# A graph layer's edge sums: groups owned by their middle edge, sums in two parts, Newton steps on ScalarE

## The chip, the cores and the metric

The kernel runs on one core of one Trainium2 chip. The metric is the device time of one launch in microseconds, as the median of several runs. A core has five engines with a queue each: TensorE (PE, with its weight loads shown apart as PEld), VectorE (DVE), ScalarE (ACT), GpSimd (POOL) and SyncE (SP, which issues DMAs). Each works its queue strictly in the order in which the program wrote it, and waits where the next instruction is not ready. DMAs are issued from SP, ACT or POOL.

## The reference, cut to what matters

There are 625 nodes of 512 features, 20,625 edges sorted by their target node (10,000 random edges in both directions, and a loop on each node), and 4 kinds of edges with a 512x512 matrix each.

```python
h = max(layernorm(x), 0)                       # 625 x 512
for r in range(4):
    w_r = where(edge_type == r, edge_weight, 0)
    total_msg += (h[src] @ W_rel[r] + b_rel[r]) * w_r[:, None]
agg = segment_sum(total_msg, dst)              # sum over the edges of each target
deg = segment_sum(edge_weight, dst)
agg = agg / max(deg, 1)[:, None]
z   = h + (h @ W_self + b_self + agg)
x1  = layernorm(z) * ln1_g + ln1_b
ffn = gelu(x1 @ W_ffn1 + b_ffn1) @ W_ffn2 + b_ffn2     # 512 -> 1024 -> 512
out = x + layernorm(x1 + ffn) * ln2_g + ln2_b
```

## The kernel before

**Blocks and the table.** The nodes stand in five blocks of 128 rows (0 to 4), 640 rows for 625 nodes; the 15 rows too many are a gap at the end of block 1 (rows 241 to 255), which so has 113 nodes. The first stage makes a table of 4 x 640 rows in memory: each block's transposed h times each kind's matrix, plus the bias (`table_rows`, matmuls at L404, the copy out of PSUM with its scale at L417, the store at L419). An edge's message is then one row of this table times its weight. While TensorE does this, VectorE works out columns of indices and weights (`outer_columns`, `group_columns` L757, `degree_columns`), one-hot tiles for the degrees, and for block 0 and part of block 4 the cells of a count matrix, which POOL scatters to memory (L687).

**Two ways to sum edges.** Blocks 0 and 4 (the outer ones) have a dense matrix of edge weights, node by table row (`sums_w`); their sums are 20 matmuls with it each, L1302, where the table comes back in chunks by DMAs from SP (`chunk_load`, L1297). The rest of block 4's matrix is made by `outer_sum` (L614), whose banks VectorE and ScalarE empty (L557 to L567). The blocks 1 to 3 and the tiles at the boundaries to the outer blocks gather rows: an indirect DMA on POOL (`gather`, L1159) brings 128 table rows for 128 edges into one of ten buffers `ms`.

**Groups of three.** Of the gathered tiles, 90 form 30 groups of three (`EG` = 3): partition p of a group's three tiles holds three consecutive edges, which nearly always have the same target. The group's owner is the target of its first edge. ScalarE scales the first row (`first_row`, L1165, into one of two PSUM buffers `add`), VectorE adds the second and the third, each with its weight where its target is the owner's, else with zero (`row_added`, L1183, weights `wgt_g` from L761). So three gathered tiles cost one product with a one-hot matrix, which takes the 128 sums to their nodes (`edge_sum`, L1201). The nine single tiles go straight from `ms` into a product, with the weight in their one-hot matrix (L1194).

**Two forms of a product.** A whole product takes fp32 operands; it shows as two matmul instructions. Where `parted` (L1175) says so, the sum is cut in two: a high part in fp32r, cast on ScalarE (`high`, L1169), and the rest as a low part, on VectorE (`low`, L1173); TensorE then does two fp32r matmuls, one behind the other, as one step of the order (L1205, L1206). Before the change that is the first two of every three groups of a set, but for the last three units of the last set.

**Stray rows.** At the border between two nodes a group can hold edges of both. An edge that is not the owner's is left out by its zero weight, and added by itself: up to two for each node, so two gathers for each of the blocks 1 to 3 (`gather_first`, L1214, six in all). `first_edges`, `first_rows` and `first_found` (L794 to L824) find them; VectorE adds these rows to z directly (`add_first`, L1211, the instruction is at L430).

**Sets, and the order.** The gathered tiles fall in sets by the blocks that they reach, in this order: (3,4) and (0,1) with 4 single tiles each; (1) with 8 groups; (1,2) with 2; (2) with 9; (2,3) with 2; (3) with 9 groups and one single tile. Each set has one PSUM accumulator `acc`, which VectorE adds to z at its end (L430). When a block's sums are complete, its norm runs (`first_norm`: L881 to L893; the inverse root by a guess and three Newton steps on VectorE, `rsqrt_steps`, L869 and L870, for block 3 by a power on POOL), its x1 is turned by TensorE (L352) and copied by ScalarE (L1365), and its feed-forward follows (`up` L925, gelu L931, `down` L945, a second norm L955 to L970, the store L996 and L998). The blocks go through it in the order 0, 4, 1, 2, 3. `self_part` (L442) is the h @ W_self of each block.

**What sets the order.** From the table's end on, the program lists operations with an engine, an estimated time, what they come after, and counted buffers that they take and give back (class `Plan`). A list scheduler in the program gives each engine a fixed order from it; at run time only the waits decide. The constants `MS`, `ES`, `OW`, `LAND` and the like are buffers and estimates of that plan. `spin` (L1226) are empty matmuls that keep TensorE's clock up.

## Time and profile before

| | us |
|---|---|
| median of 3 runs | 259.0 (258.2 to 260.4) |
| the profiled execution | 258.17 |
| its span | 256.3 |
| granted TensorE clock, mean | 0.998 |
| table stage (TensorE on L404) | 9.9 to about 84 |
| gathers issued on POOL | 88 to 222, 99 and 6 |
| feed-forward of block 3 and the end | 233.5 to 256.3 |

The span runs from the first to the last instruction of one execution. An engine's busy time counts its instructions; a TensorE that is busy isn't always at its peak. Where a row shows brackets, they hold the idle time of the engine just ahead of it and what ended it. In groups, the numbers behind the bar are busy us and the mean ns of one, then the idle time ahead.

### The profile page before, as it was taken

Reading aid. Unit: us, or ns where it says so; the run is one execution under the profiler, and the core shown is the slowest. Engines: PE = TensorE matmul, PEld = TensorE weight load, DVE = VectorE, ACT = ScalarE, POOL = GpSimd, SP = SyncE. Lnnn points to the kernel's source line nnn. Section 1 sums busy time; section 2 is a strip of 40 time slices with the busy share of each in tenths; the row PEclk is TensorE's granted clock in tenths of the full one; section 3 lists DMA queues with packets and bytes.
Section 4 is the critical chain, followed back from the end, with each engine's and each line's share of the span. In section 5 each row is a group of like instructions: output and inputs, shape, how many; then the busy total and the mean of one; then the engine's idle time right before and its main releaser. Section 6 shows DMA issues by size and latency. Waiting matters only on the chain.

```text
span 256.3 us, 3522 instructions
## 1 busy us (share of the span) xinstructions
PE 243.2 (95%) x1051; PEld 140.0 (55%) x1051; DVE 199.6 (78%) x501; ACT 79.3 (31%) x236; POOL 170.6 (67%) x230
## 2 busy tenths in 40 slices
PE   7999999999999979999995999999899999999993
PEld 6354444445445644444442445875775766847872
DVE  3797899998899974646968879997969999776232
ACT  3117400000032463713231314571542451502500
POOL 4378888888888477777777777777777777501000
PEclk9999999999999999999999999999999999999999
DMA  6999999882172399799999887677777776720101
GB/s 205 320 405 415 377 393 400 289 337 79 51 247 89 110 374 388 207 306 320 372 309 375 285 263 205 191 209 215 208 214 220 235 206 194 214 79 0 45 0 45
DMA packets 24055, 60.20 MB, mean 235 GB/s; under 512 B 4401, under 2 KB 8753, under 8 KB 22882
## 3 DMA queue, kind: packets, MB, share of 16 engines
q0 software_dynamic: 9936, 27.58, 34.9%
q1 hardware_dynamic: 13808, 30.94, 32.8%
q10 hardware_dynamic: 290, 1.44, 1.7%
q8 instruction: 9, 0.15, 0.2%
q14 instruction: 12, 0.10, 0.1%
HBM read 50.78 MB, written 9.17 MB: 234 GB/s over the span
## 4 chain that ended last, share of the span: by engine, by line
PE 54%; DMA 26%; DVE 9%; issue 4%; ACT 2%; POOL 1%; SPq 1%; POOLq 0%; DVEq 0%; ACTq 0%
PE ps L404 22%; DMA ms<-table,row_i 17%; PE ps L925 8%; PE acc L1302 6%; PE ps L945 5%; PE acc L1208 4%; PE ps L442 3%; DMA wr<-in_L_gnn_W_rel_dram 2%; DMA sums_w<-cells 2%; DMA ms<-table,x_row 2%; DVE add L1183 2%; PE spin L1226 2%; POOL ms L1159 1%; DMA cells<-weight,cell 1%; PE add L787 1%
## 5 line engine op out<-in xcount | busy, mean ns | idle before, releaser
L1159 POOL DMA_INDIRECT ms<-table,row_i x99 | 96.3, 972 | 30.9 <-issue 14.0
L404 PE MATMUL ps<-wr,hT 128*128 128x512 f32 (+2 forms) x168 | 71.2, 576 | 0.2 <-DMA wr<-in_L_gnn_W_rel_dram 0.2
L687 POOL DMA_INDIRECT cells<-weight,cell x45 | 48.3, 1073 | 9.0 <-issue 6.3
L404 PEld LDWEIGHTS ps<-wr,hT 128*128 128x128 f32 x168 | 30.7, 191 | 34.0 <-issue 30.4
L1183 DVE SCALAR_TENSOR_TENSOR add<-ms,wgt_g,add 128x512 f32<-128x512 f32 x51 | 38.0, 748 | 5.8 <-DMA ms<-table,row_i 3.1
L925 PEld LDWEIGHTS ps<-x1T,w_sb 128*128 128x128 f32 x320 | 37.3, 191 | 4.7 <-issue 2.4
L925 PE MATMUL ps<-x1T,w_sb 128*128 128x128 f32 (+2 forms) x320 | 37.8, 275 | 1.3 <-ACT x1T L1365 1.2
L1165 ACT ACTIVATE add<-ms,ed 128x512 f32<-128x512 f32 x30 | 20.7, 691 | 51.5 <-DMA ms<-table,row_i 42.3
L945 PE MATMUL ps<-w_sb,gT 128*128 128x512 f32 (+3 forms) x96 | 36.2, 522 | 0.0
L600 ACT ACTIVATE ohw<-os,w 128x128 fp32r<-128x128 f32 x36 | 11.3, 389 | 56.1 <-DVE os L582 56.1
L1302 PE MATMUL acc<-tr,sums_w 128*128 128x512 f32 x60 | 27.9, 595 | 0.0
L945 PEld LDWEIGHTS ps<-w_sb,gT 128*128 128x128 f32 (+1 forms) x96 | 16.6, 188 | 14.2 <-issue 11.4
L442 PE MATMUL ps<-ws_sb,hT 128*128 128x512 f32 x40 | 18.6, 592 | 0.0
L931 ACT ACTIVATE gT<-ps,bf 128x128 f32<-128x128 f32 (+1 forms) x40 | 13.9, 364 | 11.0 <-PE ps L925 10.1
L1302 PEld LDWEIGHTS acc<-tr,sums_w 128*128 128x128 f32 x60 | 11.0, 189 | 11.5 <-issue 10.5
L1173 DVE TENSOR_TENSOR el<-add,eh 128x512 fp32r<-128x512 f32 x21 | 14.3, 683 | 2.8 <-ACT eh L1169 2.8
L1169 ACT CAST eh<-add 128x512 fp32r<-128x512 f32 x21 | 12.2, 582 | 12.5 <-DVE add L1183 11.2
L1205 PE MATMUL acc<-eh,oh 128*128 128x512 f32 x21 | 13.2, 628 | 0.5 <-DVE z L430 0.5
L417 DVE SCALAR_TENSOR_TENSOR tr<-ps,rx,brel_bc 128x512 f32<-128x512 f32 x15 | 11.1, 743 | 3.0 <-PE ps L404 3.0
L442 PEld LDWEIGHTS ps<-ws_sb,hT 128*128 128x128 f32 x40 | 7.6, 190 | 8.0 <-issue 7.7
L1206 PE MATMUL acc<-el,oh 128*128 128x512 f32 x21 | 8.8, 418 | 2.9 <-DVE el L1173 2.8
L955 DVE TENSOR_TENSOR ow<-ps,z 128x512 f32<-128x512 f32 (+3 forms) x6 | 3.6, 596 | 10.2 <-PE ps L945 10.1
(215 smaller groups left out, 301.4 us busy)
## 6 DMA issues: line engine op xcount, KB each, us to landing
tr<-table SPq DMA_DIRECT2D x11, 512.0 KB, 6.6
w_sb<-in_L_gnn_W_ffn_dram SPq DMA_DIRECT2D x2, 2048.0 KB, 10.2
table<-tr SPq DMA_DIRECT2D x15, 256.0 KB, 6.2
wr<-in_L_gnn_W_rel_dram SPq DMA_DIRECT2D x3, 1024.0 KB, 9.5
cells<-zeros SPq DMA_DIRECT2D x2, 1280.0 KB, 11.2
ms<-table,row_i POOLq DMA_INDIRECT x99, 3.8
rows<-in_rows_dram SPq DMA_DIRECT2D x1, 1536.0 KB, 13.1
sums_w<-cells ACTq DMA_DIRECT2D x1, 1280.0 KB, 6.5
```

What stands on the lines that cost most here:

```text
L404: nc.tensor.matmul(p_[:, :h.stop - h.start], hT[i][:, k, :], wr_sb[r][:, k, h], start=(k == 0), stop=(k == KD - 1))
L442: nc.tensor.matmul(p[0], hT[i][:, k, :], ws_sb[:, k, :], start=(k == 0), stop=(k == KD - 1))
L687: s = nc.gpsimd.indirect_dma_start(out=cells[i][:, :], out_offset=bass.IndirectOffsetOnAxis(ap=cell[i][:, k:k + 1], axis=0), in_=weight[i] ...
L925: nc.tensor.matmul(pu[:, :nn + first], w1_sb[:, k, f * P:(f + 1) * P], x1T_b()[:, k, :nn + first], start=(k == 0), stop=(k == KD - 1))
L931: nc.scalar.activation(box["gT"][:, f, :nn], pus[f][:, :nn], AF.Gelu, bias=bf1[:, f:f + 1])
L945: nc.tensor.matmul(po[h][:n, :w], box["gT"][:, f, at], w2_sb[:, f, c], start=(f == 0), stop=(f == KF - 1))
L1159: nc.gpsimd.indirect_dma_start(out=ms[j], out_offset=None, in_=table[:, :], in_offset=bass.IndirectOffsetOnAxis(ap=row_i[:, j:j + 1], axis=0))
L1165: nc.scalar.activation(box["sum"], ms[j], AF.Copy, scale=wgt[:, j:j + 1])
L1173: nc.vector.tensor_sub(box["low"], box["sum"], box["high"].bitcast(F32))
L1183: nc.vector.scalar_tensor_tensor(to, ms[j], wgt_g[:, k, q - 1:q], box["sum"], op0=ALU.mult, op1=ALU.add)
L1205: nc.tensor.matmul(acc[bs], ohs[0][:, q, :], box["high"], start=(k == 0), stop=False)
L1302: nc.tensor.matmul(acc[b,], sums_w[b][:, c, :], kept[(b, c) if (b, c) in kept else c], start=first, stop=last)
```

## The change

1. **The owner of a group is its middle edge's target.** The weights `wgt_g` now exist for all three rows, zero where a row's target is not the middle's. At a border inside a group only the first or only the last row is then a stray one, so there is one stray row per border: one gather per block, three in all, chosen by `chosen`. The degree columns keep the old, first-edge owner (`wgt_1`).
2. **A block's stray rows are a tile of their own set.** Each of (1), (2), (3) begins with them: the row with its weight in two parts, times a one-hot matrix `x_hots` made in `first_found`. The direct additions to z are gone.
3. **The gap moves** to rows 255 to 269: block 1 has 127 nodes, block 2's begin at its row 14. The sets become (1) 9 groups, (1,2) 2, (2) 8, (2,3) 2, (3) as before. The feed-forward works on all 128 rows of each block.
4. **Most sums go in two parts:** all of every set but the last, single tiles too (`high_of_row`, `low_of_row`, straight from `ms`); of the last set every second unit, but for its last three. A whole sum's third addition writes into its `ms` buffer.
5. **The products of the parts are steps of their own in the plan,** and any order between the first and the last of a set is allowed. High and low parts get rings of their own (4 and 3 buffers, in place of 7 shared ones); the ring `ow` goes from 5 to 4.
6. **Newton steps:** in the first norm of blocks 0, 1, 2 and 4, and in the second of blocks 0, 4, 1 and 2, the three steps are on ScalarE, three instructions each; the guess stays on VectorE.

```diff
-        self.gap_at = 2 * P - self.gap
+        self.gap_at = 2 * P - 1
-        self.size = [P - (self.gap if b == 1 else 0) for b in range(nb)]
+        self.rows = [(self.gap - 1 if b == 2 else 0, P - (b == 1)) for b in range(nb)]
...
     def group_columns():
         first = grouped(dst_f)[:, :, 0:1].to_broadcast([P, GROUPS, EG - 1])
-        nc.vector.scalar_tensor_tensor(wgt_g, grouped(dst_f)[:, :, 1:], 0.0, first, op0=ALU.add, op1=ALU.not_equal,
+        middle = grouped(dst_f)[:, :, EG // 2:EG // 2 + 1].to_broadcast([P, GROUPS, EG])
+        nc.vector.tensor_tensor(wgt_1, grouped(dst_f)[:, :, 1:], first, op=ALU.is_equal)
+        nc.vector.tensor_mul(wgt_1, wgt_1, grouped(wgt)[:, :, 1:])
+        nc.vector.scalar_tensor_tensor(wgt_g, grouped(dst_f), 0.0, middle, op0=ALU.add, op1=ALU.not_equal,
                                        accum_out=x_missing)
-        nc.vector.tensor_tensor(wgt_g, grouped(dst_f)[:, :, 1:], first, op=ALU.is_equal)
-        nc.vector.tensor_mul(wgt_g, wgt_g, grouped(wgt)[:, :, 1:])
+        nc.vector.tensor_tensor(wgt_g, grouped(dst_f), middle, op=ALU.is_equal)
+        nc.vector.tensor_mul(wgt_g, wgt_g, grouped(wgt))
...
         nc.tensor.matmul(first[:, :INNER], before, counts[:, 1:], start=True, stop=False)
+        nc.tensor.matmul(first[:ep.rows[2][0], 1:2], behind, counts[:, 2:3], start=False, stop=False)
...
+        nc.vector.scalar_tensor_tensor(x_step, x_cols[:, :, :, 2], float(NP), x_cols[:, :, :, 0], op0=ALU.mult, op1=ALU.add)
+        chosen(x_row, x_step, x_one[:, 0, :])
+
+    def chosen(to, of, t):
+
+        nc.vector.tensor_sub(t, of[:, :, 0], of[:, :, 2])
+        nc.vector.tensor_mul(t, t, x_on[:, :, 0])
+        nc.vector.tensor_add(to, t, of[:, :, 2])
+
+    def first_found():
+
+        dst, t, ok = (x_one[:, i, :] for i in (1, 2, 3))
+        chosen(dst, x_cols[:, :, :, 1], t)
+        nc.vector.tensor_max(ok, x_on[:, :, 0], x_on[:, :, 1])
...
+        chosen(t, x_edges[:, :, :, 3].bitcast(F32), x_one[:, 0, :])
+        nc.vector.tensor_mul(x_one[:, 0, :], t, ok)
+        nc.vector.tensor_tensor(x_hots, dst.unsqueeze(2).to_broadcast([P, INNER, P]),
+                                node_row[:, :P].unsqueeze(1).to_broadcast([P, INNER, P]), op=ALU.is_equal)
...
         def improve(three):
             v, y, a = col(0), col(1), col(2)
+            if on == "ACT":
+                nc.scalar.activation(a, y, AF.Square)
+                nc.scalar.activation(a, a, AF.Copy, scale=v, bias=-three)
+                nc.scalar.activation(y, a, AF.Copy, scale=y)
+                return
...
-    ES = 7
+    EH, EL = 4, 3
-    OW = 5
+    OW = 4
-    PARTED = 2, 3
+    WHOLE = 3
+    POW, ROOTS = 0.9, (("ACT", "ACT", "ACT", "POOL", "ACT"), ("ACT",) * 5)
...
     def parted(bs, k, units):
-        return len(units[k]) > 1 and k % PARTED[1] < PARTED[0] and (k + 3 < len(units) or bs != order_of[-1])
+        return (k % 2 == 0 and k + WHOLE < len(units)) or bs != order_of[-1]
...
+    def high_of_row(j, ms, box):
+        box["high"] = buffer("eh")
+        nc.scalar.activation(box["high"], ms[j], AF.Copy, scale=weight_of(j))
+
+    def low_of_row(j, ms, box):
+        box["low"] = buffer("el")
+        nc.vector.scalar_tensor_tensor(box["low"], ms[j], weight_of(j), box["high"].bitcast(F32),
+                                       op0=ALU.mult, op1=ALU.subtract)
...
         if q == EG - 1 and not parts:
-            to = edge.tile([P, D], F32, tag="es", name=f"es_{j}", bufs=ES)
-        nc.vector.scalar_tensor_tensor(to, ms[j], wgt_g[:, k, q - 1:q], box["sum"], op0=ALU.mult, op1=ALU.add)
+            to = ms[j]
+        nc.vector.scalar_tensor_tensor(to, ms[j], wgt_g[:, k, q:q + 1], box["sum"], op0=ALU.mult, op1=ALU.add)
...
+    def products(bs, passes, last, q, ohs, box, j, needs, give, rank):
+
+        for part in ("high", "low") if "low" in needs else ("sum",):
+            first = not passes
+            passes.append(op("PE", 0.87 if part == "sum" else 0.235,
+                           lambda first=first, part=part, end=last and part != "high": edge_sum(
+                               bs, first, end, q, ohs, lambda: box[part] if part in box else ms[j]),
+                           after=[needs[part], needs["hots"], *(passes if last and part != "high" else passes[:1])], take=["acc"] if first else [],
+                           give=give[part], lag=0.25, rank=rank, level=0.25))
+        return passes[-1]
...
-        for b in range(1, NB - 1):
-            if bs == ((b, b + 1) if b < NB - 2 else (b,)):
-                for q in range(EG - 1):
-                    g_last = op("POOL", GATHER, lambda b=b, q=q: gather_first(b, q, ms), after=[g_last, rows_of_first],
-                                take=["ms"], lag=LAND, order=True, rank=(0, n))
-                    adds[b].append(op("DVE", 0.75, lambda b=b, q=q: add_first(b, q, ms), after=[g_last, first_ready],
-                                      give=[("ms", g_last)], lag=SLACK, rank=(0.3, n), level=0.05))
+        passes, k0 = [], 0
+        if len(bs) == 1:
+            b, box, rank = bs[0], {}, (0, n)
+            g_last = op("POOL", GATHER, lambda b=b: gather_first(b, ms), after=[g_last, rows_of_first], take=["ms"],
+                        lag=LAND + late(n), order=True, rank=rank)
+            high_op = op("ACT", 0.69, lambda b=b, box=box: high_of_row(-b, ms, box), after=[g_last, first_ready], take=["eh"],
+                         lag=SLACK, rank=rank)
+            h = op("DVE", 0.75, lambda b=b, box=box: low_of_row(-b, ms, box), after=[high_op], take=["el"], give=[("ms", g_last)],
+                   lag=0.6, rank=rank, level=0.7)
+            products(bs, passes, False, b - 1, [x_hots], box, None, dict(high=high_op, low=h, hots=first_ready),
+                     dict(high=[("eh", high_op)], low=[("el", h)]), rank)
...
-        steps = first_norm(z[:, b, :], b, got, pool_pow=(b == inner[-1]))
+        steps = first_norm(z[:, b, :], b, got, halves=(b == inner[-1]), root=ROOTS[0][b])
```

154 lines of the change are left out of this document (86 added, 68 removed).

## The prediction

> **What bounds the kernel now.** I read the busy time by stretches first, then the busy times and the shares of the chain that ended last on the page. The columns of the first two rows are the stretch, its length, busy us and instructions of PE, PEld, DVE, ACT and POOL, the granted clock, the DMA share and GB/s.
>
> ```profile
> 120.00:140.00 20.00, 17.09 (x55) 7.26 (x53) 16.42 (x34) 5.12 (x10) 15.24 (x16) 1.00 0.94 338
> 140.00:160.00 20.00, 20.00 (x52) 9.74 (x53) 17.48 (x31) 6.94 (x11) 15.13 (x17) 1.00 0.81 258
> ...
> PE 243.2 (95%) x1051; PEld 140.0 (55%) x1051; DVE 199.6 (78%) x501; ACT 79.3 (31%) x236; POOL 170.6 (67%) x230
> ...
> PE 54%; DMA 26%; DVE 9%; issue 4%; ACT 2%; POOL 1%; SPq 1%; POOLq 0%; DVEq 0%; ACTq 0%
> ```
>
> The reader is to see that from 140 us on TensorE has no free time, that VectorE is close behind (17.5 of 20), and that ScalarE has two thirds of its time free. Next, the chain in order of time near the end, and two idle spots in TensorE's timeline:
>
> ```profile
> 228.34 5.15 PE ps L945 x12
> 233.49 0.44 PE ps L352 x4
> ...
> 139.93 0.50 PE L1206 MATMUL acc<-el,oh 128*128 128x512 f32 x1 [2.75 <-DVE el L1173]
> ...
> 181.82 1.16 PE L925 MATMUL ps<-x1T,w_sb 128*128 128x128 f32 x8 [1.16 <-ACT x1T L1365]
> ```
>
> TensorE runs block 2's down matmuls until 233.49, turns block 3's x1 at once, and everything after that is a fixed tail. Its idle spots after 139 us are few; the largest, 2.75, is a product that waits for its own low part. The third reading is the queue of the gathers on POOL and what the last of them feeds:
>
> ```profile
> 88.45 0.98 POOL L1159 DMA_INDIRECT ms<-table,row_i  x1 [1.03 <-ACT ohw L600]
> ...
> 129.30 0.95 POOL L1216 DMA_INDIRECT ms<-table,x_row  x1 [0.30 <-issue]
> 130.55 0.95 POOL L1216 DMA_INDIRECT ms<-table,x_row  x1 [0.30 <-issue]
> ...
> 221.20 0.94 POOL L1159 DMA_INDIRECT ms<-table,row_i  x1 [0.30 <-DVE el L1173]
> ...
> 231.39 0.88 DVE L893 SCALAR_TENSOR_TENSOR z<-ow,rs_z,rows 128x256 f32<-128x256 f32 x2 [0.47 <-POOL rs_z L345]
> ...
> 213.73 0.58 ACT L1365 COPY x1T<-ps 128x512 f32<-128x512 f32 x1
> ...
> 215.87 5.92 PE L925 MATMUL ps<-x1T,w_sb 128*128 128x128 f32 x48
> ```
>
> The 105 gathers go out without a break: (221.20 - 88.45) / 104 = 1.28 us each. Block 3's x1 is ready at 231.39 + 0.88 = 232.27, 1.2 us before TensorE takes it up at 233.49; block 2's turned x1 is there at 214.31, 1.6 us before its feed-forward starts at 215.87. So three routes lie within 1.6 us of each other: TensorE's total work, the gathers up to block 3, the gathers up to block 2. A gain must come on all three.
>
> **The change, part by part.** Prices first; the columns are line, engine, operation, tiles, shape, count, busy us and mean ns of one, then idle time before. The chain's three rows give the true step of a product, since the starts of lone matmuls are modelled.
>
> ```profile
> L1205 PE MATMUL acc<-eh,oh 128*128 128x512 f32 x21 | 13.2, 628 | 0.5 <-DVE z L430 0.5
> L1208 PE MATMUL acc<-es,oh 128*128 128x512 f32 x18 | 9.4, 603 | 0.2 <-DVE es L1183 0.2
> L1208 PE MATMUL acc<-ms,oh 128*128 128x512 f32 x18 | 8.9, 606 | 1.6 <-issue 1.6
> ...
> 157.00 0.24 PE acc L1205
> 157.23 0.23 PE acc L1206
> ...
> 160.90 0.86 PE acc L1208 x2
> ...
> L1173 DVE TENSOR_TENSOR el<-add,eh 128x512 fp32r<-128x512 f32 x21 | 14.3, 683 | 2.8 <-ACT eh L1169 2.8
> L1169 ACT CAST eh<-add 128x512 fp32r<-128x512 f32 x21 | 12.2, 582 | 12.5 <-DVE add L1183 11.2 <-DVE mv_z L332 1.3
> L1165 ACT ACTIVATE add<-ms,ed 128x512 f32<-128x512 f32 x30 | 20.7, 691 | 51.5 <-DMA ms<-table,row_i 42.3 <-DVE el L1173 4.5 <-DVE es L1183 2.6
> L430 DVE SCALAR_TENSOR_TENSOR z<-ms,x_on,z 128x512 f32<-128x512 f32 x5 | 3.8, 758 | 4.4 <-DMA ms<-table,x_row 4.4
> L1194 DVE TENSOR_SCALAR oh<-node_row,dst_mod,ed 128x128 f32<-128x128 f32 x8 | 2.2, 339 | 0.0
> L1197 DVE TENSOR_TENSOR oh<-fl,node_row 128x512 fp32r<-128x512 f32 x6 | 4.1, 678 | 0.0
> L869 DVE SCALAR_TENSOR_TENSOR rs_z<-rs_z 128x1 f32<-128x1 f32 x12 | 2.5, 212 | 0.0
> L870 DVE SCALAR_TENSOR_TENSOR rs_z<-rs_z 128x1 f32<-128x1 f32 x12 | 2.0, 164 | 0.4
> L468 ACT ACTIVATE lim<-node_row 128x1 f32<-128x1 f32 x62 | 6.0, 194 | 0.0
> L930 ACT ACTIVATE bf<-ps,bf 128x1 f32<-128x1 f32 x8 | 2.1, 260 | 1.9 <-PE ps L925 1.8
> ```
>
> *Products on TensorE.* Before: 21 sums in two parts at 0.24 + 0.23 = 0.47, and 18 whole (36 instructions in the two L1208 rows, two each) at 0.86: 9.9 + 15.5 = 25.4 us. After, by the new rule and the new tile sets: the 8 single tiles at the outer boundaries, 21 groups ahead of the last set, 4 groups in it and 3 stray tiles go in two parts (36), and 5 groups and 1 single tile stay whole (6): 16.9 + 5.2 = 22.1. TensorE saves 3.3 us, all of it in the stretch where it has no free time.
>
> *Stray rows.* Six gathers become three: POOL's queue gets shorter by 3 x 1.25 (130.55 - 129.30) = 3.75 us for block 3. Up to block 2's last gather there are 73 instead of 75: 2.5 us. The seven additions of those rows on VectorE (the x5 row, and two halves of one, the price not depending on rows) go: -5.3 us. What stays is three tiles that go the way of a product (counted above and below).
>
> *High and low parts.* 15 more: 4 group sums (ACT 0.58, DVE 0.68) and 11 tiles taken straight from the gathered rows (ACT 0.69, DVE 0.75, prices of the L1165 and the x_on rows): ACT +9.9, DVE +11.0. The weighted hots of the 8 single tiles (0.34 each) become two plain ones of 0.68: DVE -1.4. A gathered buffer is now held until the low part or, for a whole sum, until its product; with ten buffers and 1.28 per gather there are 12.8 us for it, and I cost this at nothing, the cover being that POOL never waits above 0.3 us for a buffer now.
>
> *Newton steps.* Eight norms leave VectorE: 8 x 3 x (0.212 + 0.164) = -9.0 us. On ScalarE each step is a square with plain scale and two copies with a column as scale: 0.194 + 2 x 0.260 = 0.71, three steps 2.1, eight norms +17 us, in an engine with room for it. A norm's own latency gets longer by 2.1 - 1.1 = 1.0 us (bounds 0, where VectorE's queue held the steps apart, and 2 where ScalarE's queue does); it is on a path only for block 2. The Trainium skill, ScalarE: Activation LUTs, Rules for kernel authors, says multiplies and adds belong on VectorE; by that rule the move costs the 1.0 us. The same page (What ACT_TABLE_LOAD costs) gives 186 ns plus about 93 for each column operand; with it a step is an estimated 0.74 and a norm 2.2, which changes nothing here; the two ScalarE rows agree with it to within 20 ns.
>
> *Work ahead of the gathers.*
>
> ```profile
> 64.56 0.75 DVE L417 SCALAR_TENSOR_TENSOR tr<-ps,rx,brel_bc 128x512 f32<-128x512 f32 x1 [1.15 <-PE ps L404]
> ...
> 68.94 0.38 PE L797 MATMUL ps<-counts,before 128*128 128x3 f32 x2 [0.39 <-DVE counts L850]
> ...
> 88.68 0.16 DVE L823 TENSOR_REDUCE x_found<-x_on 128x1 f32<-128x6 f32 x1
> 88.87 0.16 DVE L824 TENSOR_TENSOR x_missing<-x_missing,x_found 128x1 f32<-128x1 f32 x1
> ```
>
> The group columns get 8 more small VectorE instructions, about 1.3 us at 0.1 to 0.2 each; VectorE's next idle time, 1.15 at 64.56, takes most of it. One more small product in the search of the first edges: TensorE and all after it +0.4 us (the L797 row). Behind the last table row VectorE gets about 16 more small instructions at 0.19 from start to start and the 128x384 hots of the stray rows (0.5): +3.6 us between 84 and 95 us, ahead of the hots that the bank sums on TensorE need. TensorE waits there anyway for the first gathered rows, so this costs from 0 to 3.6; I take 1.3, nearer the low end since the bank sums concerned are few.
>
> *Products laid out apart* remove the wait for a low part: between 0 and 2.75 us; I take half, 1.4, because other low parts will be late (VectorE is the next resource) though a high part of another sum can now go ahead. The smaller ring of work buffers, the buffers of their own for the parts and the moved gap I cost at nothing: the feed-forward of block 1 gets wider, but its matmuls are bound by the same step, and one copy on VectorE goes.
>
> **The sum.** VectorE: -5.3 - 1.4 - 9.0 + 11.0 + 3.6 = -1.1 us, no relief worth counting. TensorE's route: -3.3 + 0.4 + 1.3 - 1.4 = -3.0, so block 3's turn moves from 233.49 to 230.5. Gather route: 232.27 - 3.75 + 0.4 = 228.9, earlier, so not the bound. Block 2's route: 214.31 - 2.5 + 0.4 + 1.0 = 213.2 against TensorE's 215.87 - 3.0 = 212.9: level. The span goes from 256.3 to 253.3. The profiled execution took 258.17 (1.87 around its span), 0.8 below the median of 259.0; 3.0 off gives 255.2 against the one and 256.0 against the other, and I forecast 255.6.
>
> **The rivals.** *No gain to be seen.* Block 2's route binds: the longer norm costs 2 instead of 1, the work at 84 to 95 us costs its full 3.6, and TensorE's saving is spent in waits: -3.3 + 0.4 + 3.6 - 1.4 = -0.7, so 257.9. For it: 1.6 us of slack is little. Against: single tiles are cheaper on TensorE just there.
>
> *Slower: the two PSUM buffers of the group sums.* A buffer is held from a group's first row on ScalarE to its low part on VectorE; the first and the last of the 21 such holds are
>
> ```profile
> 103.48 0.67 ACT L1165 ACTIVATE add<-ms,ed 128x512 f32<-128x512 f32 x1
> 108.73 0.67 DVE L1173 TENSOR_TENSOR el<-add,eh 128x512 fp32r<-128x512 f32 x1
> ...
> 213.10 0.69 ACT L1165 ACTIVATE add<-ms,ed 128x512 f32<-128x512 f32 x1 [2.59 <-DMA ms<-table,row_i]
> 220.20 0.69 DVE L1173 TENSOR_TENSOR el<-add,eh 128x512 fp32r<-128x512 f32 x1
> ...
> L1413 ACT ACT_TABLE_LOAD x1 | 1.3, 1283 | 0.0
> ```
>
> 5.9 and 7.8 us, with a mean of 7.1 over all 21. Three gathers take 3.84, so two buffers allow 7.7 per group. Now a third of the groups hold theirs shorter; after the change 21 in a row hold it fully, and Newton steps can stand ahead of the cast. If the mean rises to 8.5, groups come every 4.25 and the 21 of them lose 21 x 0.4 = 8.6 us: 255.6 + 8.6 = 264. It decides from 7.7 on. Against it: a hold is long now because it waits for the group's other rows; started late, it shortens.
>
> *Slower by table loads.* If the square were in another table than the gelu, each of 24 squares could bring two loads of 1.28: up to 61 us on ScalarE, 280 or more. Copies, identities and gelus share one table in the trace (the two loads stand at the ends). The Trainium skill, ScalarE: Activation LUTs, Table sets: the hidden batching unit, says that cheap functions stand in every set, and names relu, copy, identity and abs, not the square.
>
> *More gain.* All waits of TensorE go (another 2.7 with the early ones): the gather route then binds at 228.9, span 251.7, time 254.0.
>
> **How the numbers follow.** About 1% is what a measurement can tell, so faster begins below 256.4. Forecast 0.50 (254 to 257, most of it below 256.4), more gain 0.10, no gain to be seen 0.24, buffers 0.13, table loads 0.03. Faster 0.52: 0.42 of the forecast's 0.50 and the 0.10. Same 0.33: the rest of the forecast, the no-gain case and a hold just beyond its point. Slower 0.15: the remainder. The range holds the first three cases: from 252.0 (the more-gain case less the 2 us that cover its early waits) to 260.0 (the no-gain case with block 2's norm one or two later).
>
> **What would show it.** 36 high and 36 low products, at 0.23 each; three gathers of stray rows; a last gather near 217.9; block 3's x1 turned near 230.5 directly behind block 2's down matmuls; no wait of TensorE for a low part; ScalarE near 106 us busy with two table loads; VectorE near 198. The forecast is wrong if TensorE shows idle stretches above 2 us behind 140 us, if POOL waits for buffers, if first rows on ScalarE wait for low parts more than now (4.5 us), or if the gathers start later than 89 us.

## The result, and the profile after

The changed kernel takes 257.1 us (median of 7 runs, 256.3 to 257.7), the kernel before 259.0 in the runs beside it. By the medians that is 1.9 us (0.7%), by the means 2.6 us: a ratio of 0.990, with an interval of 0.986 to 0.994. The forecast was 255.6 with a range of 252 to 260. The gain is real and 0.7 to 1%, 1.5 us smaller than predicted. By the forecast's own bound (faster begins below 256.4) it falls under "same", which had 0.33 against the 0.52 of "faster". The profiled execution took 256.33 with a span of 254.5, 1.8 less than the 256.3 of before.

One thing has to be known to read the numbers further down. In the runs of the experiments the engines stood still with nothing to wait for, mostly for 1 to 5 us at a time and once for 12.8, the granted clock of TensorE was 0.89 to 0.94 on the mean (0.998 in the profiles of before and after), and every kernel, the one before too, took 300 to 328 us. So each experiment is compared only with the kernel before on the same chip, or with another kernel of the same group. Each ratio is taken between the means of two kernels' runs without those that are over 1.5% slower than the fastest of their kernel, so it need not be the quotient of the medians beside it.

First the page of the changed kernel: busy times, and the shares of the chain that ended last.

```profile
PE 240.1 (94%) x1059; PEld 141.6 (56%) x1059; DVE 201.8 (79%) x480; ACT 104.1 (41%) x323; POOL 168.7 (66%) x227
...
PE 31%; DMA 30%; DVE 27%; issue 5%; ACT 2%; POOL 2%; SPq 0%; POOLq 0%; DVEq 0%; ACTq 0%
```

The chain of before was 54% TensorE; now TensorE, the transfers and VectorE share it about equally. It is still one chain, which passes through all three by turns. The end of the same chain:

```profile
211.92 5.45 DMA ms<-table,row_i
...
219.75 1.10 PE acc L1260 x2
...
225.18 5.15 PE ps L983 x12
230.33 0.44 PE ps L356 x4
```

Block 3's turn stands at 230.33, directly behind block 2's last down matmuls, where it stood at 233.49: 3.16 us earlier, against the 3.0 that were predicted (230.5). Ahead of 219.75 the chain runs over the gathers' transfers and VectorE's sums and not along TensorE; only the last 10.6 us to the turn are TensorE's own. The chain of before leaves TensorE at the same place (219.74), but there TensorE has 0.13 us of idle time from 210 us to the turn, and now 1.18. The gathers on GpSimd and the x1 of block 3 that the last of them feeds (timelines of POOL and VectorE):

```profile
88.39 1.36 POOL L1200 DMA_INDIRECT ms<-table,row_i  x1 [0.74 <-DVE od L596]
...
99.16 1.14 POOL L1275 DMA_INDIRECT ms<-table,x_row  x1 [0.30 <-DVE el L1228]
...
143.03 0.95 POOL L1275 DMA_INDIRECT ms<-table,x_row  x1 [0.30 <-DVE add L1236]
...
182.83 0.95 POOL L1275 DMA_INDIRECT ms<-table,x_row  x1 [0.30 <-DMA ms<-table,row_i]
...
218.19 1.05 POOL L1200 DMA_INDIRECT ms<-table,row_i  x1 [0.30 <-issue]
...
228.23 0.88 DVE L932 SCALAR_TENSOR_TENSOR z<-ow,rs_z,rows 128x256 f32<-128x256 f32 x2 [0.47 <-POOL rs_z L349]
```

Three gathers of stray rows in place of six, an unchanged start and pace, the last gather 3.0 us earlier (221.20 to 218.19), and x1 ready at 228.23 + 0.88 = 229.11, 1.2 us ahead of TensorE's turn. The products, by kind (count, then smallest, median and largest duration in ns), and the two rows of table loads on ScalarE:

```profile
L1260 PE MATMUL acc<-eh,oh x33: 387/477/798, 97.5 to 216.5; 128*128 128x512 f32 x33
L1260 PE MATMUL acc<-el,oh x33: 388/502/799, 100.7 to 219.1; 128*128 128x512 f32 x33
L1260 PE MATMUL acc<-ms,oh x12: 592/592/697, 198.2 to 224.6; 128*128 128x512 f32 x12
L1260 PE MATMUL acc<-eh,x_hots x3: 468/475/742, 114.6 to 197.4; 128*128 128x512 f32 x3
L1260 PE MATMUL acc<-el,x_hots x3: 394/397/476, 115.1 to 197.7; 128*128 128x512 f32 x3
...
L1087 ACT ACT_TABLE_LOAD x1 | 1.3, 1283 | 1.2 <-PEq L1594 1.2
L1482 ACT ACT_TABLE_LOAD x1 | 1.3, 1283 | 0.0
```

36 high, 36 low, 6 whole sums of two matmuls, two table loads: as laid out in the prediction. Where TensorE's time went shows best in the stretch from 84 us to the turn, in two parts (stretch, length, busy us and count of PE, PEld, DVE, ACT, POOL; before, then after):

```profile
84.00:140.00 56.00, 51.37 (x160) 24.67 (x158) 40.04 (x99) 22.10 (x51) 40.58 (x44) 1.00 0.86 305
140.00:233.49 93.49, 91.49 (x425) 59.22 (x426) 79.61 (x173) 36.49 (x80) 63.65 (x66) 1.00 0.69 205
```

```profile
84.00:140.00 56.00, 54.37 (x181) 28.85 (x180) 48.68 (x117) 30.97 (x71) 42.99 (x47) 1.00 0.91 322
140.00:230.33 90.33, 86.51 (x415) 57.23 (x414) 72.76 (x133) 50.97 (x137) 61.36 (x64) 1.00 0.68 195
```

Over both parts the 3.16 us are 1.98 of busy time and 1.18 of idle time (6.63 to 5.45). But the two parts go opposite ways. Ahead of 140 us TensorE idles 3.0 us less (4.63 to 1.63) and so gets 3.0 us more of its work done; behind 140 us it has 5.0 us less to do and idles 1.8 us more (2.00 to 3.82). The waits for a low part are nearly gone, but waits for the cast that makes a high part have come (the view of waits: us in total, times, longest):

```profile
PEld acc L1260 <- ACT eh L1210: 7.6, 7, 2.4
...
PE acc L1260 <- ACT eh L1210: 3.6, 4, 1.5
```

The longest of them, in ScalarE's and TensorE's timelines:

```profile
184.06 0.19 ACT L901 ACTIVATE rs_y<-rs_y 128x1 f32<-128x1 f32 x1
184.28 0.29 ACT L902 ACTIVATE rs_y<-rs_y 128x1 f32<-128x1 f32 x1
184.61 0.29 ACT L903 ACTIVATE rs_y<-rs_y 128x1 f32<-128x1 f32 x1
184.94 0.20 ACT L901 ACTIVATE rs_y<-rs_y 128x1 f32<-128x1 f32 x1
...
186.43 0.72 ACT L1224 ACTIVATE eh<-ms,x_one 128x512 fp32r<-128x512 f32 x1 [0.63 <-DMA ms<-table,x_row]
187.05 1.05 ACT L1210 CAST eh<-add 128x512 fp32r<-128x512 f32 x2
```

```profile
187.67 0.50 PE L1260 MATMUL acc<-eh,oh 128*128 128x512 f32 x1 [1.55 <-ACT eh L1210]
```

The cast at 187.05 stands in ScalarE's queue behind the high part of a stray row (L1224), and that one waits 0.63 us for its own transfer after two Newton steps of another norm are done. So it is the stray row's late transfer that holds this cast, not the steps. Of the four casts only one comes directly behind Newton steps:

```profile
208.64 0.29 ACT L903 ACTIVATE rs_y<-rs_y 128x1 f32<-128x1 f32 x1
208.84 0.57 ACT L1210 CAST eh<-add 128x512 fp32r<-128x512 f32 x1
```

TensorE waits 0.51 us for that one. The other two waits (0.87 and 0.69) are for casts behind first rows that waited 4.00 and 3.34 us for their gathered rows. A Newton step costs ScalarE 184.94 - 184.06 = 0.88 us from start to start, where the prediction took 0.71 and the planner 0.62.

So 3.16 us were gained at the turn, but only 1.84 reached the end of the span. What was lost lies behind VectorE's last instruction, in the last two output stores. The last 8 us of the two spans, with VectorE's last row and the view of the transfers (busy share and GB/s in 40 slices of 0.2 us; then the queue of instruction blocks, q8, with packets, MB and share). Before:

```profile
250.87 0.88 DVE L970 SCALAR_TENSOR_TENSOR ow<-ow,rs_y,xs 128x320 f32<-128x320 f32 x2
...
GB/s 0 0 0 0 0 0 0 0 0 0 0 0 41 0 0 0 0 0 0 32 333 428 208 296 15 0 0 19 13 23 23 4 0 0 0 0 0 0 0 0
...
out_dram<-ow SPq DMA_DIRECT2D x1, 160.0 KB, 3.3
```

And after:

```profile
247.71 0.88 DVE L1008 SCALAR_TENSOR_TENSOR ow<-ow,rs_y,xs 128x320 f32<-128x320 f32 x2
...
GB/s 0 0 0 0 0 41 0 0 0 0 0 0 0 252 402 266 310 78 20 23 0 0 0 6 6 13 6 23 27 0 0 0 0 0 0 0 0 0 41 0
...
q8 instruction: 1, 0.02, 1.5%
...
out_dram<-ow SPq DMA_DIRECT2D x1, 160.0 KB, 4.2
```

Both move the bulk of the stores in about 1 us and then trickle at 4 to 27 GB/s until the last packets are out; after the change the trickle is longer, and the 160 KB store lands 4.2 us after its issue in place of 3.3. From VectorE's end (251.75 and 248.59) to the end of the span it is 4.5 us before and 5.9 after. This difference of 1.4 us is what the experiments had to explain as well as the parts of the change.

### The profile page after: what moved, and what is told of

The parts are those of the page before. It is cut to its first block, busy times and chain, and to the rows that moved or that the text cites. A ratio compares the mean times of both kernels' runs of the same rounds, so it can differ in the third digit from the quotient of the medians.

```text
span 254.5 us, 3624 instructions
## 1 busy us (share of the span) xinstructions
PE 240.1 (94%) x1059; PEld 141.6 (56%) x1059; DVE 201.8 (79%) x480; ACT 104.1 (41%) x323; POOL 168.7 (66%) x227
## 4 chain that ended last, share of the span: by engine, by line
PE 31%; DMA 30%; DVE 27%; issue 5%; ACT 2%; POOL 2%; SPq 0%; POOLq 0%; DVEq 0%; ACTq 0%
DMA ms<-table,row_i 24%; PE ps L408 12%; PE ps L983 7%; DVE add L1236 4%; PE ps L963 4%; DVE tr L421 3%; PE acc L1260 3%; DMA table<-tr 3%; PE acc L1370 2%; DVE el L1214 2%; DVE same L677 2%; POOL ms L1200 2%; DMA xs<-in_x_dram 2%; DVE oc L784 2%; PE spin L1285 2%
## 5 line engine op out<-in xcount | busy, mean ns | idle before, releaser
L1236 DVE SCALAR_TENSOR_TENSOR add<-ms,wgt_g,add 128x512 f32<-128x512 f32 x55 | 40.5, 750 | 9.2 <-DMA ms<-table,row_i 7.4
L963 PE MATMUL ps<-x1T,w_sb 128*128 128x128 f32 (+1 forms) x320 | 39.0, 275 | 0.0
L983 PE MATMUL ps<-w_sb,gT 128*128 128x512 f32 (+2 forms) x96 | 36.4, 522 | 0.0
L1206 ACT ACTIVATE add<-ms,wgt_g 128x512 f32<-128x512 f32 x30 | 20.7, 689 | 34.5 <-DMA ms<-table,row_i 25.8
L983 PEld LDWEIGHTS ps<-w_sb,gT 128*128 128x128 f32 x96 | 16.7, 190 | 13.5 <-issue 10.8
L1260 PE MATMUL acc<-eh,oh 128*128 128x512 f32 x33 | 17.5, 540 | 3.8 <-ACT eh L1210 3.6
L1260 PE MATMUL acc<-el,oh 128*128 128x512 f32 x33 | 19.4, 604 | 0.3 <-DVE el L1214 0.3
L1214 DVE TENSOR_TENSOR el<-add,eh 128x512 fp32r<-128x512 f32 x25 | 16.8, 684 | 2.7 <-ACT eh L1210 2.6
L969 ACT ACTIVATE gT<-ps,bf 128x128 f32<-128x128 f32 x40 | 13.8, 363 | 4.7 <-PE ps L963 3.5
L1260 PEld LDWEIGHTS acc<-eh,oh 128*128 128x128 f32 x33 | 6.2, 189 | 11.8 <-ACT eh L1210 7.6
(238 smaller groups left out, 308.6 us busy)
```

Of the source, the lines that this page charges most:

```text
L963: nc.tensor.matmul(pu[:, :nn + first], w1_sb[:, k, f * P:(f + 1) * P], x1T_b()[:, k, :nn + first], start=(k == 0), stop=(k == KD - 1))
L983: nc.tensor.matmul(po[h][:n, :w], box["gT"][:, f, at], w2_sb[:, f, c], start=(f == 0), stop=(f == KF - 1))
L1206: nc.scalar.activation(box["sum"], ms[j], AF.Copy, scale=wgt_g[:, (j - GROUP0) // EG, 0:1])
L1214: nc.vector.tensor_sub(box["low"], box["sum"], box["high"].bitcast(F32))
L1236: nc.vector.scalar_tensor_tensor(to, ms[j], wgt_g[:, k, q:q + 1], box["sum"], op0=ALU.mult, op1=ALU.add)
L1260: nc.tensor.matmul(acc[bs], w.bitcast(F32) if of.dtype == F32 else w, of, start=first, stop=last)
```

## The experiments

The theory from the two profiles: the shorter products and the shorter waits of TensorE moved the turn, the gathers are 1.2 us behind as the next bound, and 1.4 us were given back at the end. The rivals: the Newton steps on ScalarE cost the missing time; the products are not what moved the turn; laying the products apart did nothing; the end is chance. The chain above speaks for one more, which no run tests: three gathers fewer bring the gathered rows 3 us earlier, and that moved the turn.

**The changed kernel once more**, nothing edited.

> The changed kernel once more, nothing edited. 256.3 to 257.7 us. The profile after gained 3.16 us at block 3's turn (233.49 to 230.33) but only 1.84 in the span, because the time from VectorE's last instruction to the span's end was 5.90 against 4.55. If that is part of the change, it is 5.9 here too, and close to 4.55 in no profile of this kernel; if it is the spread of one execution, it falls anywhere from 4.5 to 6.

Measured 308.6 us against 309.8 of the kernel before beside it (0.996 by the medians; its runs scatter from 300 to 310, and an interval was not to be had). What slowed everything shows first on VectorE, in the midst of small instructions that wait for nothing ("issue"), and then on TensorE (timelines of this run):

```profile
45.43 0.33 DVE L734 TENSOR_TENSOR lim<-lim,shift 128x162 f32<-128x162 f32 x1 [2.35 <-issue]
...
51.26 0.98 PE L801 MATMUL add<-oc,w 128*4 128x21 bf16 x26 [4.07 <-DVE oc L784]
52.16 9.70 PE L408 MATMUL ps<-wr,hT 128*128 128x512 f32 x16
```

TensorE waits 4.07 us for VectorE, and its next 16 matmuls take 9.70 us, where they took 7.13 in the profile after:

```profile
47.21 7.13 PE L408 MATMUL ps<-wr,hT 128*128 128x512 f32 x16
```

The stretches of 20 us show the same further on (the clock is the column before the last two; profile after first, then this run):

```profile
140.00:160.00 20.00, 20.00 (x84) 12.23 (x83) 17.82 (x31) 11.94 (x30) 15.12 (x17) 1.00 0.73 209
```

```profile
140.00:160.00 20.00, 12.33 (x39) 5.79 (x37) 11.46 (x21) 6.55 (x16) 10.74 (x11) 0.83 0.72 229
```

With TensorE idle for more than a third of such a stretch, this run says nothing on the 3.16 us. It does answer the question of the end, where few instructions are left: VectorE ends at 300.81 + 0.88 = 301.69, the span at 307.6, 5.9 us again. The loss at the end belongs to the kernel.

**Newton steps back on VectorE.** All orders are laid out anew by the planner.

```diff
-    POW, ROOTS = 0.9, (("ACT", "ACT", "ACT", "POOL", "ACT"), ("ACT",) * 5)
+    POW, ROOTS = 0.9, (("DVE", "DVE", "DVE", "POOL", "DVE"), ("DVE",) * 5)
```

> The changed kernel with all Newton steps back on VectorE (block 3's first norm stays on GpSimd, as before). My theory: TensorE's own work sets the turn, the move of the steps is worth nothing either way: turn 230 to 231, 256.5 to 257.7 us. Rival 1: ScalarE's Newton chains stand ahead of the casts and make TensorE wait (1.55 us at 187.67, 0.87 at 139.08, 0.69 at 216.46, 0.51 at 209.46); then these waits go, the turn comes at 228.5 to 229.5 and the time is 255 to 256. Rival 2: VectorE needs the relief (some 9 norms by 0.8 us of small steps, 7 us more on VectorE); then the last gather comes after 219.5, the turn after 231.5, and the time is over 258.3.

304.6 us, 0.985 of the kernel before (0.981 to 0.989). The median is 4 us under that of the changed kernel on the same chip, but the changed kernel's fastest run (300.1) is under every run of this one, so the two are not told apart. In the profiled executions VectorE ends at 301.80, in the run above at 301.69: no difference shows up to there, and the whole 1.8 us between the spans (305.8 and 307.6) lies in the end, which is 4.0 us here and not 5.9. VectorE's busy time went from 201.2 to 207.4 us without a visible price.

**The parts as before**: two of three groups in two parts, single tiles whole except the stray ones.

```diff
-        return (k % 2 == 0 and k + WHOLE < len(units)) or bs != order_of[-1]
+        return len(units[k]) > 1 and k % 3 < 2 and (k + 3 < len(units) or bs != order_of[-1])
```

> The changed kernel with the rule of before for what is summed in two parts: two of three groups, no single tile but the three stray ones. By the sum of the prediction 12 products go from 0.47 back to 0.86 us: TensorE +4.7 us of work. My theory, TensorE's work sets the turn: turn at 234 to 235, 260.5 to 262 us. Rival, the gathers set it and TensorE has slack: the turn moves by the 1 us or so that the routes are apart, and then TensorE is level: 257 to 259 us, with less idle time of TensorE between 84 us and the turn than the 5.45 of now.

308.3 us, 0.993 (0.988 to 0.998), its median level with the changed kernel's 308.6 on that chip; VectorE ends at 301.27, the end takes 5.9 us. The 4.7 us that the extra whole products were to cost are not to be seen. On a TensorE that is stopped for many times that, this is weak evidence. And the order is another one: all 16 down matmuls of block 2 now stand behind block 3's turn, where the changed kernel has them ahead of it, so that the turn (275.98) can't be compared with a forecast for the old order:

```profile
276.97 7.03 PE L983 MATMUL ps<-w_sb,gT 128*128 128x512 f32 x16
```

The run fits the rival, but it doesn't measure the slack of an undisturbed run.

**High and low product as one step**, laid out anew.

```diff
+        if "low" in needs:
+            def both(first=not passes):
+                edge_sum(bs, first, False, q, ohs, lambda: box["high"])
+                edge_sum(bs, False, last, q, ohs, lambda: box["low"])
+            passes.append(op("PE", 0.47, both, after=[needs["high"], needs["low"], needs["hots"], *(passes if last else passes[:1])],
...
+            return passes[-1]
```

> The changed kernel with the high and the low product of a sum laid out as one step, directly one behind the other, as before the change; everything else stays. My theory (the prediction's 1.4 us for laying them out apart): the waits for a low part are back (2 to 4 us in all in the waits of TensorE), turn at 231.2 to 232.2, 258 to 259 us. Rival: the wait for a low part went with the other parts of the change, and laying out apart is worth nothing: turn 230 to 230.8, 256.5 to 257.7 us.

319.4 us, 1.032 (1.026 to 1.037). This looked like a large price of the joined form. Because the runs were disturbed, the two last kernels were taken again on another chip:

> Again the changed kernel with the rule of before for what is summed in two parts (two of three groups, no single tile but the three stray ones), since in the first run of it every engine of every kernel, the kernel before too, stood still for stretches of 2 to 10 us that no edit explains. By the sum of the prediction 12 products go from 0.47 back to 0.86 us: TensorE +4.7 us of work. My theory, TensorE's work sets the turn: turn at 234 to 235, 260.5 to 262 us where the kernel before takes 259. Rival, the gathers set it and TensorE has slack: turn at 230.5 to 232.5, 257 to 259 us, with less idle time of TensorE between 84 us and the turn than the 5.45 of the changed kernel.

> Again the changed kernel with the high and the low product of a sum laid out as one step. My theory (the prediction's 1.4 us for laying them out apart): TensorE waits 2 to 4 us more in all for low parts, turn at 231.2 to 232.2, 258 to 259 us where the kernel before takes 259. Rival 1: laying out apart is worth nothing: turn 230 to 230.8, 256.5 to 257.7 us. Rival 2, from the disturbed first run (3.2% over the kernel before): it is worth far more than was reckoned, the turn comes at 234 or later, because high buffers are held until the low product and the casts behind them start late: then ScalarE's casts wait for products of TensorE, and the time is over 260.

314.2 us, 1.007 (0.998 to 1.015), and 324.3 us, 1.017 (1.009 to 1.024); the kernel before took 316.0 there. And a third time, with the Newton steps, on a third chip:

> Once more the changed kernel with the high and the low product of a sum laid out as one step, in the hope of a chip on which the kernel before takes 259 us and not 310 to 316. My theory (the prediction's 1.4 us for laying them out apart): TensorE waits 2 to 4 us more in all for low parts, turn at 231.2 to 232.2, 258 to 259 us. Rival 1: worth nothing: turn 230 to 230.8, 256.5 to 257.7 us. Rival 2, from two disturbed runs (3.2% and 1.7% over the kernel before): worth far more, turn at 234 or later, over 260 us, with ScalarE's casts held until a low product has given a buffer back.

> Once more the changed kernel with all Newton steps back on VectorE (block 3's first norm stays on GpSimd). My theory: TensorE's own work sets the turn, the move is worth nothing either way: turn 230 to 231, 256.5 to 257.7 us where the kernel before takes 259. Rival 1: ScalarE's Newton chains stand ahead of the casts and make TensorE wait; without them the turn comes at 228.5 to 229.5 and the time is 255 to 256 (the disturbed run points this way: 1.5% under the kernel before). Rival 2: VectorE needs the relief (some 7 us of small steps more): last gather after 219.5, turn after 231.5, over 258.3 us.

323.8 us, 1.024 (1.013 to 1.035), and 310.9 us, 0.972 (0.962 to 0.981), the kernel before at 316.1. No chip was undisturbed. But the joined form was slower each time, and TensorE's timeline at its end, on the third chip, says why:

```profile
277.32 1.48 PE L1292 MATMUL spin<-zeros 128*128 128x256 bf16 x10
283.00 1.09 PE L356 MATMUL ps<-ident,z 128*128 128x128 f32 x4 [4.20 <-DVE z L932]
284.54 1.11 PE L356 MATMUL ps<-ident,z 128*128 128x128 f32 x4 [0.46 <-DVE z L932]
286.33 9.15 PE L963 MATMUL ps<-x1T,w_sb 128*128 128x128 f32 x64 [0.67 <-ACT x1T L1440]
```

Both turns, block 2's and block 3's, stand behind the last sum; TensorE idles 4.2 us ahead of them and then has two whole feed-forwards to do, where the changed kernel does most of block 2's between the sums. The edit changed the planner's step from 0.235 twice to 0.47 once, and with it the whole order. These three runs measure an order, not the wait for low parts.

So the last runs kept the changed kernel's order and edited only what each step issues.

**The Newton steps in place**, on VectorE at the places that the planner had given them on ScalarE:

```diff
-            if on == "ACT":
-                nc.scalar.activation(a, y, AF.Square)
-                nc.scalar.activation(a, a, AF.Copy, scale=v, bias=-three)
-                nc.scalar.activation(y, a, AF.Copy, scale=y)
-                return
```

> The changed kernel with its order of instructions kept as it is, but each Newton step that it issues on ScalarE issued at the same place on VectorE, as two instructions (in the earlier runs with the steps on VectorE the whole order was laid out anew). My theory: ScalarE's chains cost about 1 us (three steps took 2.65 us, the planner reckoned 1.86, and four waits of TensorE for a cast follow them, 3.6 us in all, of which the gathers' route leaves 1 us to be won): 0.3 to 0.6% under the changed kernel. Rival 1: level within 0.2%. Rival 2: VectorE's 27 steps of 0.3 us more, 8 us, make it slower by 0.5% or more.

**The products joined in place**: the high one issued directly ahead of its low one.

```diff
+        def issue(first, part, end):
+            if part == "high":
+                held.append(first)
+                return
+            if held:
+                edge_sum(bs, held[0], False, q, ohs, lambda: box["high"])
+            edge_sum(bs, first, end, q, ohs, lambda: box[part] if part in box else ms[j])
```

> The changed kernel with its order of instructions kept, but each high product issued only at the place of its low product, directly ahead of it (in the earlier runs of the joined form the whole order was laid out anew, and block 2's feed-forward came to stand behind the last sum, with TensorE idle for 4 us ahead of it, so that they tell nothing of the products). My theory: TensorE waits in all 1 to 2 us more for low parts, and the time rises by 0.3 to 0.8% against the changed kernel. Rival: since a high product waits for nothing but a low part some 1.4 us later, the work behind it moves up and nothing is lost, within 0.2%.

**No filler products** around block 3's feed-forward; nothing reads what they compute.

```diff
     def spin(n):
+        return
```

> The changed kernel without the 30 filler products on zeros that TensorE runs around block 3's feed-forward (spin; nothing reads them), the order of all else kept. In the profile after, one 16 KB block of instructions is fetched (queue q8) at 249.7 us, in the middle of the last two output stores, as TensorE comes to the end of its last 25 fillers at 249.0; the stores trickle to the end and VectorE's last instruction stands 5.9 us before the end of the span. In the runs so far it stood 5.9, 5.9 and 5.7 us before it where a block was fetched during the stores, and 3.5, 3.5 and 3.5 where none was. My theory, the fetch holds the stores up: without the fillers TensorE is done 3 to 4 us earlier, the block is fetched ahead of the stores, and the distance falls to 3.4 to 4.0; the time falls by 2 us against the changed kernel. Rival: the stores' landing varies for reasons of its own, the distance stays between 4.5 and 6, and the time stays.

All three on one chip, the kernel before at 309.6 (the changed kernel unedited was not run there): the steps in place 306.3 us, 0.990 (0.985 to 0.995); the products joined in place 308.0 us, 0.990 (0.982 to 0.997); no fillers 304.1 us, 0.985 (0.979 to 0.991). The first two intervals lie on each other, and on the 0.990 that the unedited kernel has in the result. The predicted price of joining (0.3 to 0.8%) and the predicted gain of the steps (0.3 to 0.6%) are both within the scatter: neither shown nor excluded by these runs.

The third overlaps them too, so that the 2 us under the changed kernel that were expected of it are not shown either.

The fillers decide the question of the end. VectorE's last row and the view of the last 8 us without them:

```profile
297.69 0.88 DVE L1008 SCALAR_TENSOR_TENSOR ow<-ow,rs_y,xs 128x320 f32<-128x320 f32 x2
...
GB/s 0 0 0 0 0 0 0 0 0 0 0 0 0 0 0 41 0 0 0 0 0 0 41 90 320 333 304 234 27 4 0 0 0 0 0 0 0 0 41 0
...
q1 hardware_dynamic: 288, 0.26, 9.8%
q14 instruction: 3, 0.02, 1.0%
```

No q8 block is left in these 8 us, the stores run through with hardly a trickle, and from VectorE's end (298.57) to the span's (302.4) it takes 3.8 us: inside the 3.4 to 4.0 that the theory gave, outside the rival's 4.5 to 6. The same edit in the kernel before:

> The kernel before, without its 30 filler products, the order of all else kept. In its profile the 16 KB block of instructions came at 252.3 us, behind the start of the last two stores, and the span ended 4.55 us after VectorE's last instruction. My theory, a block fetched during the last stores holds them up, whatever the kernel: the block comes ahead of the stores, the distance is 3.4 to 4.0 us, and the time falls by 0.6 to 1.1 us, 0.996 to 0.998 of the kernel before. Rival, the fillers or the changed kernel's other stores matter in some other way: the distance stays at 4.3 to 4.8 us.

307.8 us against 309.5, 0.987 (0.981 to 0.992). The view of its last 8 us:

```profile
302.69 0.88 DVE L970 SCALAR_TENSOR_TENSOR ow<-ow,rs_y,xs 128x320 f32<-128x320 f32 x2
...
GB/s 0 82 0 0 0 0 0 0 0 0 0 0 0 0 0 0 0 0 0 41 0 0 0 0 0 0 0 333 397 209 338 35 0 0 0 0 0 0 0 0
```

The 82 GB/s in one slice of 0.2 us are the 16 KB block, now 5 us ahead of the stores; the end takes 306.7 - 303.57 = 3.1 us where it took 4.5. So the block came ahead of the stores as expected, and the end fell even under the 3.4 to 4.0 that the theory gave. The edit is worth more here (1.3%) than the 1.4 us of the end (0.5%), and more than the 0.2 to 0.4% expected; where the rest comes from is open.

The fillers were meant to keep TensorE's clock up. In these runs they do nothing for it that the tail shows: from the turn's first matmul (280.19 without them) to VectorE's end it is 18.4 us in the changed kernel with and without them.

The transfer records of all the traces, side by side: which blocks of instructions (16 KB on q8, 8 KB on q14) were fetched while the last two stores ran, the us from the first packet of these stores to the last, and the us from VectorE's end to the span's.

| kernel | blocks during the stores | stores | end |
|---|---|---|---|
| joined, three profiles | none | 0.9, 0.9, 0.9 | 3.5, 3.5, 3.5 |
| before, no fillers | none | 0.9 | 3.1 |
| changed, no fillers | 8 KB | 1.1 | 3.8 |
| Newton steps on VectorE, two profiles | 8 KB, and 16 KB as they end | 1.4, 1.1 | 4.0, 3.8 |
| before | 16 KB | 2.3 | 4.5 |
| changed, two profiles | 16 KB and 8 KB | 3.2, 3.2 | 5.9, 5.9 |
| parts as before, two profiles | 16 KB and 8 KB | 3.3, 3.0 | 5.9, 5.7 |
| Newton steps in place; joined in place | 16 KB and 8 KB | 3.2; 3.0 | 5.4; 5.7 |

The stores' length follows the blocks without an exception, in both kernels, in disturbed runs and undisturbed ones. The records also show how. In the seven profiles with stores of 2.3 to 3.3 us, the last 18 of their 288 packets, exactly one sixteenth where a core has 16 DMA engines, begin together as the 16 KB block's record ends (within 0.02 us); the other 270 are through after 0.9 to 1.4 us. In three of the seven the block's record begins only when those 270 are through, so what held the 18 until then isn't in the records. That the running fillers themselves slow the stores is a rival that one trace speaks against. With the Newton steps on VectorE the fillers run until 302.97, the stores from 302.35 to 303.73, and they are short all the same:

```profile
298.45 4.52 PE L1285 MATMUL spin<-zeros 128*128 128x256 bf16 x30
```

Of the 1.4 us that the change lost at the end, 0.9 are in the stores: the 16 KB block was there before the change, the 8 KB block at their start is new. Which engine it belongs to wasn't found. The other 0.4 us lie behind the stores' last packet, from which it is 1.7 us to the end of the span before and 2.1 after. Over all 14 profiles this stretch is 1.7 where the last 8 KB fetch begins after the span's end (three) and 2.0 to 2.1 where it begins 0.3 us or less ahead of it (eleven); no run tests whether the one makes the other.

## Why the prediction was right, and where it failed

- *The turn.* Predicted 230.5, measured 230.33, at the predicted place. The sum's total was right, its split was not, so that an agreement within 0.2 us is in part luck. The products were to save 3.3 us of TensorE's work behind 140 us, and the waits were to come to nothing (+1.3 - 1.4). Measured were 5.0 us less work there and 1.8 us more waiting, and 3.0 us less waiting ahead of 140 us (busy time with modelled ends is a rough measure of work). Of the terms ahead of 140 us the +0.4 came (TensorE leaves the table stage 0.5 us later, 84.23 for 83.71), the +1.3 did not: TensorE's idle time from 84 to 104 us fell from 1.6 to 0.6. Nor has TensorE "no free time" there after the change: from 210 us to the turn it waits 1.18 us, and the chain runs over the gathered rows until 219.75. The experiments couldn't tell the terms apart, because in them TensorE has idle time to swallow any of them. That the parts moved the turn, and not the three gathers fewer, is therefore argued from the profiles, not shown by a run.
- *Block 2's route.* Predicted level with TensorE, at 213.2 against 212.9. Block 2's turned x1 is ready at 209.89 and its feed-forward starts at 209.94: level, but 3 us earlier than forecast, and 5.9 earlier than before. The gain at the turn can be read off there. Behind 219.7 us TensorE has the same whole sums and down matmuls left in both kernels, but 8 up matmuls of block 2 in place of 32, and one product in two parts less: 10.6 us in place of 13.75.
- *Stray rows and gathers.* Three gathers fewer, the last at 218.19 against 217.9 expected, x1 at 229.11 against 228.9. Right, and with it the claim that block 3's x1 doesn't bind, by 1.2 us. That the gathers bind nothing else does not follow: the last products wait for them too.
- *Work ahead of the gathers.* VectorE's busy time from 80 to 100 us is 18.25 in the view by stretches against 14.6 before, the 3.6 predicted, and the gathers start at 88.39 as before (88.45).
- *VectorE near 198.* It is busy 201.8. The durations of all its instructions in the trace add up to 223.4 before and 224.4 after, +1.0 against the -1.1 of the sum, or +0.2 with the 1.3 of the group columns that the sum of VectorE had left out. The busy time rose by 2.2, because it counts overlapping instructions once. The term that this mis-sized is the Newton steps' -9.0: with the steps back in place on VectorE the durations are 9.2 us more than in the unedited kernel's run, the busy time 6.8 (201.2 to 208.0). A busy time can't be predicted by subtracting durations.
- *Newton steps.* ScalarE near 106: 104.1. A step was taken at 0.71 and takes 0.88: its three dependent instructions start 0.22, 0.33 and 0.33 us apart. The Trainium skill, ScalarE: Activation LUTs, Rules for kernel authors, has such multiplies on VectorE; the prediction read a price of 1.0 us from that. The runs neither confirm nor exclude it: VectorE's last instruction ends at 301.7 with the steps on ScalarE and 301.8 without, in one execution each, and the kernels with the steps on VectorE stand at 0.972 to 0.990 of the kernel before.
- *Laid out apart.* "No PE wait for a low part" came nearly true (0.33 us in one wait). What the prediction missed is what took their place, four waits for a cast, 3.6 us, three of them behind a row whose transfer was late and one, 0.51 us, behind Newton steps. The 1.4 us for this term is neither confirmed nor refuted.
- *The rivals.* The "add" buffers didn't bind: GpSimd never waited above 0.31 us while gathering and the first rows waited 4.1 us for low parts, under the bound of 4.5 that the prediction set. No table loads came.
- *The step that failed* is the sentence that "everything after that is a fixed tail". From the turn to VectorE's last instruction it is: 18.26 us in both. Behind it 1.4 of the 3.16 us were given back, 0.9 of them in the last two stores, which now run beside two fetches of instructions and not beside one. The pieces add up, 258.17 - 3.16 + 1.36 = 256.4, and the execution took 256.33. The two runs without fillers and the 18 late packets show the mechanism for the 16 KB block, the table makes it likely for the 8 KB one. It was not in the prediction at all, although the instruction queues stand on the page of before.

A version that beats the kernel before in the disturbed runs is the changed kernel without fillers: 0.985 (0.979 to 0.991). That it beats the changed kernel is not shown. Undisturbed it wasn't run; it should take some 2 us off the changed kernel, an estimate from the end's 5.9 against 3.8. The Newton steps on VectorE, laid out anew, stand no worse (0.985 and 0.972, also without a comparison undisturbed).

## What to carry over

A total that comes out right doesn't confirm its terms: split the stretch, and follow the new chain before saying what moved it. Look at what stands behind the last compute instruction before calling a tail fixed: the landing of the last stores depends on what else the DMA engines carry then, instruction blocks included, and work that nobody reads at the end of an engine's program can put a block there. In a kernel laid out by a planner, an experiment that edits a step's cost or shape measures a new order; keep the order and edit what a step issues. And removing a wait for one part of a pair only helps if its other part is made early: read what stands ahead of the new releaser in its engine's queue.

## What the runs showed of the hardware

A fetch of one 16 KB block of instructions (1.5% of 16 engines' 8 us in the profile after, 1.9 us on one of them) beside two output stores of 256 KB together stretches them from 0.9 to 2.3 us, and with an 8 KB block at their start to 3.0 to 3.3, with a trickle of 6 to 27 GB/s where 250 to 400 flowed before: one sixteenth of the packets goes only when the block is through. A 16 KB block that comes only as the stores end leaves them at 1.1 and 1.4 us. The Trainium skill, Runtime: NRT & Kernel Launch, Instruction fetch mechanics, says that an engine's instructions are refilled in 16 KiB blocks over a DMA queue of its own, and that crossing a boundary is "mostly hidden". The size agrees with the trace for q8 (0.02 MB each), not for q14, whose blocks have 8 KB; what is hidden from the engine is not hidden from the last stores, where one block costs 1.4 us and two cost 2.1 to 2.4.

The second surprise is the disturbance itself: TensorE's busy time rose from 240.1 to 259.7 us, 8%, but the span from 254.5 to 307.6, 21%. The lower clock looks like its companion and not its root: the first long stall in the repeated run, 2.35 us on VectorE from 43 us, comes ahead of TensorE's wait, and the slow matmuls come behind that wait. A stall of the same length stands at the same place in the first run with the Newton steps on VectorE, so its place at least is not chance. The Trainium skill, TensorE: Matmul & The Clock Gate, What's actually happening, describes a gate that is throttled by default, released by activity and closed after some 3.4 us without; the wait of 4.07 us ahead of the slow matmuls fits that, but no run here tests it. Why engines stood with nothing to wait for on every chip of the experiments, and in none of the first runs, stays open.
